# A hand-planned kernel of two attention layers on one core: side products given out by a forecast of their supply

## The chip, the cores and the metric

The kernel runs on one core of a Trainium2 chip. The core has five engines: TensorE (PE, matrix products), VectorE (DVE), ScalarE (ACT), GpSimd (POOL) and SyncE (SP, which here starts DMAs). The metric is the device time of one execution in microseconds (us), and the median of several runs counts.

## What is computed

Four images x of 256 channels and 64 x 64 pixels go through two layers. Each layer first normalizes its input in groups of eight channels and adds its result to that input.

```python
# layer 0: attention of all pixels over a half-sized grid
q = einsum('oc,bchw->bohw', Wq, x)                 # 8 heads of 32
k = conv(x, Wk, strides=(2, 2)); v = conv(x, Wv, strides=(2, 2))
attn = softmax((q.k + q.(rel_h + rel_w)) * scale)  # 4096 queries, 1024 keys
x = x + attn @ v
# layer 1: attention inside each quarter of the image
q, k, v = split(conv1x1(x, w_qkv, b_qkv))
out = softmax(q.k * scale) @ v                     # 1024 queries, 1024 keys, 4 areas
out = out + depthwise_conv7x7(v, w_pe, b_pe)
x = x + conv1x1(out, w_proj, b_proj)
```

(The lines are shortened; q, k and v stand for the normalized input's products.) All numbers are 32-bit floats.

## The kernel before, in words

**Units, steps and phases.** The work is eight blocks: layer 0 of images 0 to 3 ("A"), then layer 1 of images 0 to 3 ("B"). A block has 16 units; a unit is 512 queries of four heads (a head group, `qd` 0 or 1). A unit has 8 steps, one for each 128 of its 1024 keys: 128 units, 1024 steps. The main loop at the end of `direct_path` goes in phases of one and a half steps, 683 in all (`PHASES`). A phase does, in this order for TensorE: the score products `s` of one full step and half of another (L365); the weighted sums `av` of the phase before (L432); and between the two a place for other products. ACT makes the exponentials of the scores (L407 for a full step, two of them, and L418 for a half step), 1024 columns each. DVE adds the exponentials up for the divisors (`acc`, L442).

**PSUM.** It has eight banks. Six hold scores in three pairs (`ps_banks`). One has the tag `av` and holds the running sum of a unit; one has the tag `side` and holds whatever side product is being made (`ps_side`). When a unit's sums are complete, `evict` copies the bank out on ACT (L1055), and only then can the next unit's sums begin in it. In some phases the sums handled belong to two units; `cut` is then not zero, and the order is: sums of the old unit, its eviction, the place for side products, sums of the new unit.

**Side products.** Keys (`make_k`), values (`make_v`, `values`), queries (`make_q`), the output projection (`project`) and the depthwise convolution written as products with band matrices (`convolve`, L979) are generators, cut into parts: two parts for a product of 512 columns or for a convolution of 16 channels, four parts for a key or value product of layer 0. `task` puts one into the list `side`, with its number of parts, a due unit and a test `ready`. `choose` takes the ready task with the earliest due time; a task that has begun is ended before another is taken, since there is one bank. `advance` does one part. `need` forces a task to be done when its result is read.

**How many parts a phase gets.** `pressure` returns how many ready parts wait (`waiting`) and the largest ratio of parts to phases left before they are due (`rate`). If the sums for a unit's divisors are complete, the phase makes the divisors (`den`, L451) and nothing else. Otherwise it gives two parts (four at a rate above 2) when the phase is cut, more than nine parts wait or the rate is above 1; none when at most two wait, nothing has begun and the rate is below 1; and else one, or none, one or two at a unit's edge.

**Divisors.** After `den`, ACT copies it out, and POOL's queue sends it through memory and back twice (rows, few, recs, rb: L469 to L480), with a reciprocal on DVE in between. DVE multiplies the unit's sums by the result two units later (L483). DVE, ACT and each queue work strictly in the order of the program.

**The plan.** `at(g, j, f)` puts a call into step j of unit g. It is used for loads (SP), statistics (`add_stats`, DVE), normalizations (`later`, taken one per phase by `norm_next`, ACT), residual adds, and the calls of `task`. `plan_a` sets the times of layer 0, `plan_b` those of layer 1, `plan_values` those of the values that the convolution reads, and `plan_conv` those of the convolution. What has a negative unit runs before the loop: for image 0 the statistics, all keys and values, and the first queries, and for image 1 the loading for its statistics. There each product takes one of the score pairs, and TensorE runs through them in order. In layer 0 the keys of both head groups become visible together, when the last of the second group's products is in place and the position terms have been added (L548, L549).

**Convolution.** Each `convolve` uses two shares (a band matrix and rows of values for eight channels), loaded by `load_share` through SP's queue into tiles that earlier convolutions free (L960 and L738).

Of the kernel before, what the change touches and what calls it, by code (L numbers as in the profile page):

```python
# [60 lines left out]
def direct_path(  # L61
# [108 lines left out]
    turn = [0]  # L170
# [23 lines left out]

    def task(parts, f, *args, due, ready=None):

        side.append([parts, f(*args), False, ready, due * NKT])

# [40 lines left out]
    def later(token, f, start=0, first=False):  # L239

        if now[0] < 0:
            f()
            norm_done[token] = -1
        else:
            norms_left.insert(0 if first else len(norms_left), (token, f, start))
# [248 lines left out]
    def plan_a(b, u, prep):  # L494
# [3 lines left out]
        early = prep - (5 if b else 0)  # L498
# [13 lines left out]
        def load(a):  # L512
            fetched["a", a] = phase[0]
            areas[a] = [first[2 * a + half] if b == 0 else load_chunk(b, 2 * a + half, "xa") for half in range(2)]
# [58 lines left out]
        plan_norm(key, early + 4 if b != 1 else 0, 3 if b > 1 else 1)  # L573
        for a in range(NAREA):
            g = prep + (2 + 3.4 * a if b else 6 + 2.2 * a)
            at(0, int(NKT * (g - 2.1)), lambda a=a: load(a))
            for n in range(8):
                at(0, int(NKT * (g - 1.6)) + n, lambda a=a, n=n: later(("taps", b, a), lambda: make_taps(a, n), fetched["a", a] + 4))
            for n in range(2):
                at(0, int(NKT * (g + 0.6 * n)), lambda a=a, n=n, g=g: task(4, make_k, a, n, due=min(g + 3.5, u), ready=normed("taps", b, a)))  # L580
                at(0, int(NKT * (g + 0.6 * n + 1.2)), lambda a=a, n=n, g=g: task(4, make_v, a, n, due=min(g + 4, u), ready=normed("taps", b, a)))
# [3 lines left out]
        def fetch(c):  # L585
            fetched["q", c] = phase[0]
            hqs[c] = load_chunk(b, c, "hq")
# [32 lines left out]
        for c in range(NCH):  # L620
# [6 lines left out]
            for qd in range(2):  # L627
                at(g - 2, 4, lambda c=c, qd=qd, g=g: task(2, make_q, c, qd, due=g - 0.5, ready=normed("hq", b, c)))
# [7 lines left out]
                lambda: need(ks, key),  # L636
# [7 lines left out]
    def plan_b(b, u):  # L644
# [66 lines left out]
        for a in range(NAREA):  # L711
# [4 lines left out]
            for n in range(4):  # L716
                at(g - 4, 1 + 4 * n, lambda a=a, n=n, g=g: task(2, make_k, a, n // 2, n % 2, due=g - 1, ready=normed("hs", b, a)))
# [3 lines left out]
        for c in range(NCH):  # L721
            for qd in range(2):
                at(u + 2 * c - 2, 1, lambda c=c, qd=qd: task(2, make_q, c, qd, due=u + 2 * c - 0.5, ready=normed("hs", b, c // 2)))
# [74 lines left out]
        for c in range(NCH):  # L798
# [12 lines left out]
            for to in range(CT):  # L811
                at(g, j + 2, lambda c=c, to=to, g=g: task(2, project, c, to, due=g + 1.6))
# [67 lines left out]
    def plan_values(b, c, start):  # L880
# [50 lines left out]
        for t in range(CT):  # L931
            at(0, when + 7, lambda t=t: task(
                2, values, t, due=start + 2.5, ready=lambda: written[-2] + 4 <= phase[0] and normed("hv", b, c)()
            ))
# [64 lines left out]
    def plan_conv(b, n, start):  # L999
# [4 lines left out]
        def ready():  # L1004
            return all(k in loaded and loaded[k][2] + 4 <= phase[0] for k in ((b, 2 * n), (b, 2 * n + 1)))

        at(0, when, lambda: task(2, convolve, b, n, due=start + 1.5, ready=ready))
# [75 lines left out]

    f = step = 0
    before = []
    while f < PHASES or before or plan or side or quick or norms_left or to_add or to_divide:
# [17 lines left out]
        waiting, rate = pressure()  # L1104
        if due and not begun():
# [23 lines left out]
        norm_next()  # L1129
        if before:  # L1130
# [601 lines left out]
```

## Time and profile before

| | us |
|---|---|
| median of 3 runs | 3141.38 (3141.13 to 3144.78) |
| the profiled execution | 3138.1 |
| its span, first to last instruction | 3136.3 |
| TensorE busy | 3058.4 (98%) |
| VectorE busy | 2517.6 (80%) |
| ScalarE busy | 2456.8 (78%) |
| mean granted TensorE clock | 0.997 |
| the main loop's first score product | 81.6 |
| the main loop's last phase begins | 3104.1 |

The page lists busy time for each engine, groups of instructions by line with a mean duration and the idle time ahead of them, and waits by who released them. Two things are to be kept in mind. Matmuls are pipelined, and a matmul that is held up inside is drawn longer, so a busy TensorE need not be at its peak. And a share of busy time is a mean over stretches with different limits. Times in the timeline count from the span's start.

### The profile page before, as it was taken

How to read it: one execution, taken by the hardware profiler on the slowest of the kernel's cores; microseconds unless marked ns; L12 is line 12 of the kernel's file. 1: busy time of each engine (PE TensorE's matmuls, PEld its weight loads, DVE VectorE, ACT ScalarE, POOL GpSimd, SP SyncE). 2: the span in 40 equal slices, each digit the busy share in tenths (PEclk: the TensorE clock that was granted, in tenths of full speed). 3: DMA queues.
4: the chain of work that ended last, by engine and by line, in shares of the span. 5: the costliest groups of instructions: out<-in, count | busy, mean ns of one | idle time of the engine just before them, and what ended most of it. 6: DMA issues, size and time to landing. Idle time of an engine off the chain costs nothing.

```text
span 3136.3 us, 109812 instructions
## 1 busy us (share of the span) xinstructions
PE 3058.4 (98%) x47138; PEld 1247.9 (40%) x47138; DVE 2517.6 (80%) x2719; ACT 2456.8 (78%) x2988; POOL 486.4 (16%) x923
## 2 busy tenths in 40 slices
PE   7999999999999999999999999999999999999997
PEld 4344433344344444334334444443333444433332
DVE  3788888878787777878778888888887888888888
ACT  2888888888787878878877777788877777778875
POOL 0111111111111111111111111111111111111111
PEclk9999999999999999999999999999999999999999
DMA  5243444556455646566777666665666556633212
GB/s 186 55 96 80 117 97 97 119 109 152 116 155 141 172 133 166 121 158 171 197 187 189 161 173 164 156 178 126 133 130 154 141 156 173 176 103 85 65 44 70
DMA packets 648322, 423.70 MB, mean 135 GB/s; under 512 B 411772, under 2 KB 556636, under 8 KB 647832
## 3 DMA queue, kind: packets, MB, share of 16 engines
q1 hardware_dynamic: 619384, 380.11, 48.0%
q0 software_dynamic: 28448, 36.48, 4.7%
q8 instruction: 378, 6.19, 0.9%
q14 instruction: 112, 0.92, 0.1%
HBM read 318.32 MB, written 98.09 MB: 133 GB/s over the span
## 4 chain that ended last, share of the span: by engine, by line
PE 46%; issue 4%; DMA 2%; DVE 1%; ACT 1%; POOL 1%; SPq 0%; ACTq 0%; POOLq 0%; DVEq 0%
PE s L365 16%; PE av L432 13%; PE q1ps L165 4%; PE ops L165 4%; PE k1ps L165 3%; PE conv_ps L979 2%; PE den L451 2%; PE vals_ps L165 1%; DMA recs<-few 1%; DVE acc L442 1%; ACT p L407 1%; POOL rb L480 0%; SPq L738 0%; DMA xm<-xmid 0%; DMA rb<-recs 0%
## 5 line engine op out<-in xcount | busy, mean ns | idle before, releaser
L442 DVE TENSOR_TENSOR acc<-acc,p 128x1024 f32<-128x1024 f32 x1790 | 2114.1, 1220 | 448.2 <-PE av L432 188.0
L407 ACT ACTIVATE p<-s 128x1024 f32<-128x1024 f32 x1194 | 1160.1, 1025 | 455.6 <-PE s L365 441.3
L418 ACT ACTIVATE p<-s 128x1024 f32<-128x1024 f32 x598 | 620.0, 1037 | 4.0 <-issue 1.8
L365 PE MATMUL s<-q,k_A 32*64 32x256 f32 (+1 forms) x10928 | 557.8, 498 | 11.1 <-ACT p L407 8.1
L365 PE MATMUL s<-q,k_B 32*64 32x512 f32 (+1 forms) x10912 | 548.6, 497 | 2.7 <-ACT p L407 2.1
L432 PE MATMUL av<-p,v_A 128*32 128x256 f32 (+1 forms) x4784 | 455.6, 487 | 0.0
L432 PE MATMUL av<-p,v_B 128*32 128x512 f32 (+1 forms) x4776 | 451.2, 487 | 0.0
L365 PEld LDWEIGHTS s<-q,k_A 32*64 32x64 f32 x10928 | 255.9, 130 | 355.5 <-issue 129.5
L365 PEld LDWEIGHTS s<-q,k_B 32*64 32x64 f32 x10912 | 259.0, 130 | 344.6 <-issue 135.8
L480 POOL DMA_DIRECT2D rb<-recs x508 | 252.0, 502 | 522.4 <-DMA recs<-few 433.2
L478 POOL DMA_DIRECT2D recs<-few x127 | 70.0, 551 | 1394.8 <-DVE sums L477 1225.6
L432 PEld LDWEIGHTS av<-p,v_B 128*32 128x32 f32 x4776 | 148.5, 110 | 262.1 <-issue 236.5
L432 PEld LDWEIGHTS av<-p,v_A 128*32 128x32 f32 x4784 | 149.2, 110 | 241.1 <-issue 202.7
L407 ACT ACTIVATE acc<-s 128x1024 f32<-128x1024 f32 x172 | 166.9, 1023 | 78.0 <-PE s L365 77.8
L451 PE MATMUL den<-acc,ones 128*32 128x512 f32 x1024 | 147.1, 610 | 8.6 <-DVE acc L442 7.6
L470 POOL DMA_DIRECT2D few<-rows x127 | 72.3, 569 | 434.8 <-DMA rows<-den_sb 428.5
L165 PE MATMUL ops<-cv,wp_sb 128*32 128x512 f32 x1024 | 125.4, 604 | 5.2 <-DVE cv L750 4.4
L165 PE MATMUL k0ps<-taps,wkv 128*32 128x256 f32 x2048 | 124.5, 385 | 2.5 <-ACT taps L329 2.5
L165 PE MATMUL q1ps<-h,wqkv_sb 128*32 128x512 f32 x1024 | 123.8, 598 | 1.9 <-ACT q L707 1.9
L165 PE MATMUL vals_ps<-hv,wqkv_sb 128*32 128x512 f32 x1024 | 123.8, 598 | 0.2 <-ACT gmean_A L300 0.2
L165 PE MATMUL k1ps<-h,wqkv_sb 128*32 128x512 f32 x1024 | 123.5, 598 | 0.0
L165 PE MATMUL q0ps<-hq,wq_sb 128*32 128x512 f32 x1024 | 122.8, 597 | 0.0
(99 smaller groups left out, 2128.8 us busy)
## 6 DMA issues: line engine op xcount, KB each, us to landing
rows<-vals SPq DMA_DIRECT2D x384, 195.9 KB
rb<-recs POOLq DMA_DIRECT2D x508, 64.0 KB, 3.0
share<-vals SPq DMA_DIRECT2D x128, 195.9 KB
vala<-vout SPq DMA_DIRECT2D x128, 144.0 KB
vals<-vout SPq DMA_DIRECT2D x128, 144.0 KB
vc<-vala SPq DMA_DIRECT2D x64, 288.0 KB
band<-mats SPq DMA_DIRECT2D x96, 176.0 KB
hq<-in_x SPq DMA_DIRECT2D x32, 512.0 KB
```

The costliest lines, as they stand in the source:

```text
L165: T.matmul(out[cols, :], lhsT=lhsT[:, cols], rhs=rhs, start=start, stop=stop)
L365: T.matmul(out[n : n + WIDE], lhsT=unit[2]()[rows, unit[0], j * P + n : j * P + n + WIDE], rhs=unit[1]()[rows, cols], start=True, stop=True,)
L407: S.activation(p, (a, b)[n], AF.Exp, scale=SCALE)
L418: S.activation(p, c.rearrange("p b (l n) -> p b l n", l=2), AF.Exp, scale=SCALE)
L432: T.matmul(out, lhsT=v[:, j, unit[0] * P + HD * h : unit[0] * P + HD * h + HD], rhs=rhs, start=(j == 0 and not u), stop=(j == NKT - 1), sk ...
L442: V.tensor_add(to, to, p)
L451: T.matmul(dens[g][HD * h : HD * h + HD, :], lhsT=ones, rhs=p(h), start=(n == 0), stop=(n == len(sets) - 1),)
L470: G.dma_start(few[:, 0, :], rows.rearrange("h (q n) -> (h q) n", n=CH // HD))
L478: G.dma_start(recs.rearrange("h (q n) -> (h q) n", n=CH // HD), few[:, 1, :])
L480: G.dma_start(rb[HD * h : HD * h + HD, :], recs[h : h + 1, :].to_broadcast([HD, CH]))
L979: T.matmul(ps[HD * m : HD * m + HD, (2 * k + i) * size : (2 * k + i + 1) * size].rearrange("p (y x) -> p y x", y=NY), lhsT=band[:, half].r ...
```

## The change

It does the following, and leaves every product and its operands as they are.

- **Supply.** `task_at` enters each task, with the phase in which it is expected, into `upcoming`. `supply` adds up the parts that are ready or to come over each horizon of 1 to 24 phases, divides each sum by 13/16 of the phases in it, and takes the least. The loop gives two, one or no part by `credit` plus the larger of supply and rate, each up to 2; what is left over goes into `credit` (between -0.5 and 0.5).
- **Banks.** The tags `av` and `side` become `banks`, two tags; in a cut phase that gives no part and has no task begun, the two change roles.
- **Keys by head group.** The keys of layer 0 become visible for each head group by itself. Three key products of image 0's second group (12 parts) are held back and put into `side` when the loop begins, due at unit 0.6.
- **The plan.** Starting units, due times and lags of loads, statistics, taps, keys, values and convolutions change. In the first 12 phases up to two more normalizations are taken in a phase that gives more than two parts.

```diff
-    turn = [0]
+    turn, banks = [0], ["m0", "m1"]
...
-        return psum.tile([P, CH], FP, tag="side", name=name, bufs=1)
+        return psum.tile([P, CH], FP, tag=banks[1], name=name, bufs=1)
...
+    def task_at(step, parts, f, *args, due, ready=None, lag=1):
+
+        expected = [step * 2 // 3 + 1 + lag, parts]
+        upcoming.append(expected)
+
+        def give():
+            upcoming.remove(expected)
+            task(parts, f, *args, due=due, ready=ready)
+
+        at(0, step, give)
+
+    def supply():
+
+        far = 24
+        comes = [0] * (far + 1)
+        chained = 0
+        for parts, _, started, ready, _ in side:
+            if started or ready is None or ready():
+                comes[0] += parts
+            elif ready.__name__ == "chained":
+                chained += 5
+                comes[min(chained, far)] += parts
+            else:
+                comes[1] += parts
+        for when, parts in upcoming:
+            if when - phase[0] <= far:
+                comes[max(when - phase[0], 1)] += parts
+        total, least = 0, 4.0
+        for h in range(far):
+            total += comes[h]
+            least = min(least, total / max(1, (h + 1) * 13 / 16))
+        return least
...
-        early = prep - (5 if b else 0)
+        early = prep - (5 if b == 1 else 7 if b else 0)
...
-                if qd == 1:
-                    ks[key] = k
+                ks["A", b, qd] = k
...
-        plan_norm(key, early + 4 if b != 1 else 0, 3 if b > 1 else 1)
+        plan_norm(key, early + 4, 3 if b > 1 else 4 if b else 1)
         for a in range(NAREA):
-            g = prep + (2 + 3.4 * a if b else 6 + 2.2 * a)
-            at(0, int(NKT * (g - 2.1)), lambda a=a: load(a))
+            g = prep + (1 + 3.6 * a if b == 1 else 0.05 + 3.7 * a if b else 6 + 2.2 * a)
+            at(0, int(NKT * (g - 2.4)), lambda a=a: load(a))
...
+                if b == 0 and a and n:
+                    held.append((4, make_k, a, n))
+                else:
+                    task_at(int(NKT * (g + 0.6 * n)), 4, make_k, a, n, due=min(g + 3.7, u) if a < 3 or not n else u + 0.3, ready=normed("taps", b, a))
+                task_at(
+                    int(NKT * (g + 0.6 * n + 1.2)), 4, make_v, a, n, due=min(g + 4.2, u - 0.2), ready=normed("taps", b, a)
+                )
...
-                lambda: need(ks, key),
+                lambda n=n: need(ks, ("A", b, n % 2)),
...
-            plan_values(b, c, (18.4, 45.5, 54.5, 84.5)[b] + (1.7, 0.8, 1.3, 1.2)[b] * c)
+            plan_values(b, c, (18.4, 43, 52, 72)[b] + (1.7, 0.9, 1.4, 1.7)[b] * c)
         for n in range(C // 16):
-            plan_conv(b, n, (33, 55.2, 71, 97)[b] + (0.9, 0.95, 0.95, 1.0)[b] * n)
+            plan_conv(b, n, (35, 54.5, 70.5, 89)[b] + (1.2, 0.95, 1.1, 1.5)[b] * n)
...
-            av_of[g] = psum.tile([P, CH], FP, tag="av", name="av", bufs=1)
+            av_of[g] = psum.tile([P, CH], FP, tag=banks[0], name="av", bufs=1)
...
+    for parts, g, *args in held:
+        task(parts, g, *args, due=0.6)
     f = step = 0
-    before = []
+    before, credit = [], 0.0
...
-        waiting, rate = pressure()
+        _, rate = pressure()
+        parts = 0
         if due and not begun():
...
-            waiting = 0
-        elif cut or waiting > 9 or rate > 1 or due or f >= PHASES:
-            side_parts(4 if rate > 2 else 2)
-        elif waiting <= 2 and not begun() and rate < 1:
-            pass
-        elif boundary(mine):
-            side_parts(1 if begun() else 2 if waiting >= 4 else 0)
         else:
-            side_parts(1)
+            wanted = credit + max(min(supply(), 2.0), min(rate, 2.0))
+            if rate > 2:
+                parts = side_parts(4)
+            elif rate > 1.5 or due or f >= PHASES or wanted >= (0.8 if cut else 1.5):
+                parts = side_parts(2)
+            elif wanted >= 0.5 and not cut or begun():
+                parts = side_parts(1)
+            credit = max(-0.5, min(wanted - parts, 0.5))
+            if cut and not parts and not begun():
+                banks.reverse()
...
         norm_next()
+        for _ in range(max(parts, 2) - 2 if f < 12 else 0):
+            norm_next()
```

The rest of the diff turns the other calls of `task` into `task_at`, with due times that are 0.2 to 1.5 units later for most of them (`make_q`, the keys of layer 1, `project`, `values`, `convolve`), and lets what was normalized or loaded before the loop count as ready in the first phase.

More of the change, by code (lines that the diff above doesn't have):

```diff
@@ L193, in direct_path @@
     phase = [0]
+    upcoming, held = [], []
     def task(parts, f, *args, due, ready=None):
         side.append([parts, f(*args), False, ready, due * NKT])
+    def task_at(step, parts, f, *args, due, ready=None, lag=1):
[25 more added lines that the diff above has]
+        return least
     def choose():
@@ L242, in later @@
             f()
-            norm_done[token] = -1
+            norm_done[token] = -2
         else:
@@ L512, in load @@
         def load(a):
-            fetched["a", a] = phase[0]
+            fetched["a", a] = phase[0] if now[0] >= 0 else -4
             areas[a] = [first[2 * a + half] if b == 0 else load_chunk(b, 2 * a + half, "xa") for half in range(2)]
@@ L572, in plan_a @@
             at(early + c // 2, 4 * (c % 2) + (6 if b else 3), lambda c=c: add_stats(c))
-        plan_norm(key, early + 4 if b != 1 else 0, 3 if b > 1 else 1)
+        plan_norm(key, early + 4, 3 if b > 1 else 4 if b else 1)
         for a in range(NAREA):
-            g = prep + (2 + 3.4 * a if b else 6 + 2.2 * a)
-            at(0, int(NKT * (g - 2.1)), lambda a=a: load(a))
+            g = prep + (1 + 3.6 * a if b == 1 else 0.05 + 3.7 * a if b else 6 + 2.2 * a)
+            at(0, int(NKT * (g - 2.4)), lambda a=a: load(a))
             for n in range(8):
-                at(0, int(NKT * (g - 1.6)) + n, lambda a=a, n=n: later(("taps", b, a), lambda: make_taps(a, n), fetched["a", a] + 4))
+                at(0, (max(int(NKT * (g - 1.9)), 3) if b else int(NKT * (g - 1.6))) + n, lambda a=a, n=n: later(("taps", b, a), lambda: make_taps(a, n), fetched["a", a] + 4))
             for n in range(2):
-                at(0, int(NKT * (g + 0.6 * n)), lambda a=a, n=n, g=g: task(4, make_k, a, n, due=min(g + 3.5, u), ready=normed("taps", b, a)))
-                at(0, int(NKT * (g + 0.6 * n + 1.2)), lambda a=a, n=n, g=g: task(4, make_v, a, n, due=min(g + 4, u), ready=normed("taps", b, a)))
+                if b == 0 and a and n:
[5 more added lines that the diff above has]
+                )
         xcs, hqs, made_q = {}, {}, {}
         def fetch(c):
-            fetched["q", c] = phase[0]
+            fetched["q", c] = phase[0] if now[0] >= 0 else -4
             hqs[c] = load_chunk(b, c, "hq")
@@ L627, in plan_a @@
             for qd in range(2):
-                at(g - 2, 4, lambda c=c, qd=qd, g=g: task(2, make_q, c, qd, due=g - 0.5, ready=normed("hq", b, c)))
+                task_at(NKT * (g - 2) + 4, 2, make_q, c, qd, due=g - 0.3, ready=normed("hq", b, c))
             at(g + 3, 0, lambda c=c: load_residual(c))
@@ L716, in plan_b @@
             for n in range(4):
-                at(g - 4, 1 + 4 * n, lambda a=a, n=n, g=g: task(2, make_k, a, n // 2, n % 2, due=g - 1, ready=normed("hs", b, a)))
+                task_at(
+                    NKT * (g - 4) + 1 + 4 * n, 2, make_k, a, n // 2, n % 2, due=g - 0.4, ready=normed("hs", b, a)
+                )
             for n in range(4):
@@ L722, in plan_b @@
             for qd in range(2):
-                at(u + 2 * c - 2, 1, lambda c=c, qd=qd: task(2, make_q, c, qd, due=u + 2 * c - 0.5, ready=normed("hs", b, c // 2)))
+                task_at(
+                    NKT * (u + 2 * c - 2) + 1, 2, make_q, c, qd, due=u + 2 * c - 0.5, ready=normed("hs", b, c // 2)
+                )
         rest, made_x = {}, {}
@@ L811, in plan_b @@
             for to in range(CT):
-                at(g, j + 2, lambda c=c, to=to, g=g: task(2, project, c, to, due=g + 1.6))
+                task_at(NKT * g + j + 2, 2, project, c, to, due=g + (2.2 if b < B - 1 else 3), lag=0)
         return [
@@ L931, in plan_values @@
         for t in range(CT):
-            at(0, when + 7, lambda t=t: task(
-                2, values, t, due=start + 2.5, ready=lambda: written[-2] + 4 <= phase[0] and normed("hv", b, c)()
-            ))
+            task_at(
+                when + 7, 2, values, t, due=start + 4,
+                ready=lambda: written[-2] + 4 <= phase[0] and normed("hv", b, c)(), lag=1 + 4 * t,
+            )
     loaded = {}
@@ L1003, in plan_conv, with chained @@
             at(0, when - 8, lambda: len(loaded) < room and load_share(True))
-        def ready():
+        def chained():
             return all(k in loaded and loaded[k][2] + 4 <= phase[0] for k in ((b, 2 * n), (b, 2 * n + 1)))
-        at(0, when, lambda: task(2, convolve, b, n, due=start + 1.5, ready=ready))
+        task_at(when, 2, convolve, b, n, due=start + 2.5, ready=chained, lag=3)
     units = []
```

## The prediction

> **What bounds the kernel now.** I read the page's busy shares first, then PE's timeline phase by phase (a phase is one turn of the main loop: 1.5 steps of scores, exponentials and weighted sums, and what side products the loop adds), then the waits, then windows for the granted clock.
>
> ```profile
> PE 3058.4 (98%) x47138; PEld 1247.9 (40%) x47138; DVE 2517.6 (80%) x2719; ACT 2456.8 (78%) x2988; POOL 486.4 (16%) x923
> ```
>
> TensorE looks full. Is it full everywhere? PE's timeline over phases that carry two side parts (columns: start, length, engine, line, operation):
>
> ```profile
> 2235.97 1.58 PE L365 MATMUL s<-q,k_B 32*64 32x256 f32 x32
> 2237.48 1.92 PE L165 MATMUL vals_ps<-hv,wqkv_sb 128*32 128x512 f32 x16
> 2239.22 1.47 PE L432 MATMUL av<-p,v_B 128*32 128x512 f32 x16
> 2240.62 1.58 PE L365 MATMUL s<-q,k_B 32*64 32x256 f32 x32
> 2242.13 1.92 PE L165 MATMUL k1ps<-h,wqkv_sb 128*32 128x512 f32 x16
> 2243.87 1.47 PE L432 MATMUL av<-p,v_B 128*32 128x256 f32 x16
> ```
>
> From one first score product to the next: 2240.62 - 2235.97 = 4.65 us, without a gap. Now a stretch in which the loop gave out no side product:
>
> ```profile
> 473.81 2.00 PE L365 MATMUL s<-q,k_A 32*64 32x256 f32 x32 [0.17 <-ACT p L407]
> 475.74 1.50 PE L432 MATMUL av<-p,v_A 128*32 128x256 f32 x16
> 477.17 1.89 PE L365 MATMUL s<-q,k_A 32*64 32x256 f32 x32
> 478.99 1.50 PE L432 MATMUL av<-p,v_A 128*32 128x512 f32 x16
> 480.42 1.93 PE L365 MATMUL s<-q,k_A 32*64 32x256 f32 x32
> 482.27 1.50 PE L432 MATMUL av<-p,v_A 128*32 128x256 f32 x16
> 483.70 1.89 PE L365 MATMUL s<-q,k_A 32*64 32x256 f32 x32
> 486.11 1.76 PE L451 MATMUL den<-acc,ones 128*32 128x512 f32 x5 [0.52 <-DVE acc L442]
> ```
>
> These phases last 3.25 to 3.36 us. PE is drawn as busy, but the same 32 score products take 1.89 to 2.00 us, not 1.58: they are waiting inside. The first window below shows by whom: ACT is busy 13.30 of 13.30 us (and DVE 13.06). So the bound changes with the filling of a phase.
>
> ```profile
> 470.40:483.70 13.30, 13.13 (x196) 4.13 (x192) 13.06 (x13) 13.30 (x18) 2.75 (x6) 1.00 0.34 81
> 853.90:857.10 3.20, 2.04 (x36) 0.54 (x32) 3.10 (x3) 3.20 (x6) 0.00 (x0) 1.00 0.88 273
> 857.10:863.70 6.60, 4.98 (x24) 1.12 (x24) 3.13 (x6) 3.03 (x5) 1.92 (x4) 0.74 0.23 85
> ```
>
> (Columns: window, its length, busy time of PE, weight loads, DVE, ACT, POOL; granted clock, DMA share, GB/s.)
>
> I cut the whole trace into its 683 phases at the first score product. Medians: two parts 4653 ns (413 phases), one part 3799 (61), divisors and no part 3794 (127). So a part costs PE 854 ns, divisors 849, and the rest of a phase 3799 - 854 = 2945. The 66 phases with nothing should take 2945; outside the start they take 3.2 to 3.4, or 4.2 to 4.6 where one unit's sums end inside the phase ("cut"):
>
> ```profile
> 1893.02 1.58 PE L365 MATMUL s<-q,k_B 32*64 32x256 f32 x32
> 1894.53 0.64 PE L432 MATMUL av<-p,v_B 128*32 128x256 f32 x8
> 1896.67 1.07 PE L432 MATMUL av<-acc,v_B 128*32 128x512 f32 x8 [1.50 <-ACT av_sb L1055]
> 1897.66 1.58 PE L365 MATMUL s<-q,k_B 32*64 32x256 f32 x32
> ```
>
> The new unit's sums go to the bank that ACT still has to empty, and no side product lies between.
>
> I charge each phase with what it lasts above 2945 + 854 per part + 849 for divisors. That excess is 96 us of the 3136.3 us span; it is all that a better distribution could win:
> - 38.0 us in the phases without a part: 19.8 in 54 plain ones (5 at the start), 18.2 in 12 cut ones.
> - 27.2 us in phases at most three behind such a phase. Four short phases leave DVE no room (its accumulating adds take 2114 / 683 = 3.1 us a phase), so the next divisors wait for it; ACT pays its debt as 0.42 us in the next full phase.
> - 31.0 us with no empty phase near: DVE or DMA late at 1545 to 1580 us (about 8), at 405 to 430 and 498 to 510 us, ACT's eviction in one-part cuts.
>
> The dearest single wait:
>
> ```profile
> 858.70 2.10 PE L451 MATMUL den<-acc,ones 128*32 128x512 f32 x5 [2.76 <-DVE acc L442]
> ```
>
> **A rule that speaks against the change.** The Trainium skill (Perfetto Trace Analysis, "Identifying the Most-Contended Engine") says matmul occupancy is a bad measure of PE's load and that the share of weight loads should be read instead. By it PE stands at 40%, DVE at 80% is the bound, and giving out PE's work more evenly is worth about 0. The rows decide otherwise: 854 ns more for each part, in 413 phases alike, is an engine without slack. Only the empty phases obey ACT and DVE.
>
> **The change, part by part.**
>
> *Even giving out (supply, credit, expected tasks).* Parts in the loop: 948 in this trace, 12 more after the change, and the phases not used by divisors are 683 - 127 = 556: 960 / 556 = 1.73 parts each. Per 16 units (about 69 such phases), from the diff's start units, tasks that become available: 108, 128, 138, 114, 138, 132, 118, 84, so 1.2 to 2.0 a phase; no stretch is below one. A phase with one part already costs exactly PE's time (median excess 0), so "0 2 0 2" made into "1 1 1 1" gains the whole excess of the zeros. Readiness is bunched, so I leave about 12 empty phases at 0.3 to 0.4: 5 us remain of 38.0. **Gain 33.**
>
> *The debts behind empty phases*, 27.2 us. The wait at 858.70 belongs here: empty and full phases in turn up to it, then 2.76 us of waiting, and then the matmuls run at half pace (granted clock 0.74 in the window above), 6.05 us of excess in all. The skill (TensorE: Matmul & The Clock Gate, Part 1) puts the fall to half clock behind an idle window of about 3.4 us. By that rule this wait costs 2.8 us; by the row 6.0. I take the row. The pair at 1386 to 1396 us (3.2 + 1.4) I leave standing: ACT waits 4.4 us there for the load of hv, a DMA matter, and then the clock falls too. With 1.6 of others, 6 us remain. **Gain 21.**
>
> *The others*, 31.0 us. What hangs on one-part cuts, on group statistics asked for too late (phases 99 to 101 and 169, 4.8 us) and on layer 0's late four-part products (405 to 430 us, 2.9) is moved by the earlier statistics and later due times. What hangs on transposes, position adds and DMA stays. **Gain 9.**
>
> *Banks change roles* in a cut phase without a part: the 1.50 us wait falls to ACT's pace (0.36). It overlaps the 18.2 above, and is not counted twice.
>
> *A new cost.* The loop now gives out single parts more often, and a part begun must be ended before another task: some cut phases get one part, which covers the eviction badly. Two such cuts stand in the trace, excess 0.42 and 0.85. There are about 85 cuts; an eighth at 0.63: **7 us lost** (0 if none falls so, 25 if 40 do).
>
> *Keys by head group; three key products held.* Before the loop PE runs without a gap from 20.6 to 80.9 us, 3.45 us for each key or value product, so 3 x 3.45 = 10.4 us leave it; the loop gets 12 x 0.854 = 10.2. Net nothing but the filled phases 0 to 5 (3.9 us, in the 33). The second group is first read in phase 5; rate is above 2, so four parts go into each of phases 0, 1, 2. Its two position adds (1.22 each) come beside DVE's adds in phases of 6.4 us: hidden, 2.4 us if not.
>
> *Moved steps.* For images 2 and 3 eight loads of xs and sixteen statistics (0.68 each, 10.9 us of DVE) come two units earlier; the first image's convolution two units later and slower (1.2 units apart, was 0.9), so it now runs into the values of images 1 and 2; the values of images 1 and 2 come 2.5 units earlier, the last image's values 12.5 and its convolution 8. Layer 0's taps, keys and values of images 1 to 3 come one or two units earlier, so they are no longer late before their first use. Bytes stay. All go through SP's one queue, where share loads wait for their convolution (433.7 us on conv_ps L979), so whatever stands behind waits too; the POOL chain for divisors shares the DMA engines. Between 43 and 53 units the DMA share was 0.62 and will rise; at 60 to 64 it hardly changes. I take 0 net; bounds -8 (waits at 1545 to 1580 us ease) and +15 (three more waits like that of 858.70).
>
> *Extra normalizations in phases 0 to 11:* 0.6 us of ACT each in phases of over 4.6 us: nothing.
>
> Sum: 33 + 21 + 9 - 7 = **56 us**. The profiled execution took 3138.1 us (span 3136.3): 3082. The median of the runs, 3141.4, is 3.3 above it: **3085 us**.
>
> **Rivals.**
> - *DVE and DMA keep their waits (24%).* Only the empty phases go, the debts reappear where ACT, DVE or DMA are late anyway: 33 from the first, 7 from the second, -7: 3108. For it: DVE at 80% overall, 0.86 DMA share at 1540 to 1580 us. Against it: the debts sit behind empty phases.
> - *The moved plan clears the other waits too (13%).* Remaining excess about 17: 3062.
> - *Supply dries up (5%).* Tasks are listed but not ready, the rate rule saves too much or phases stay empty; only the changed banks gain 12 x 1.2: 3127.
> - *Slower (6%).* The first image's convolution, now beside values from 43 to 53 units, makes divisor chains, hv loads and shares late, and each such wait, as that of 858.70, costs 6 by the half clock. It decides from ten of them, 10 x 6 = 60 against 56 gained; with 15, one in 1.7 units, 3141 - 56 + 90 = 3175.
>
> **How the numbers follow.** Even filling 52% at 3085, own range 3070 to 3098. The 80% range takes in most of the two neighbours, 3058 to 3114; outside it are dried-up supply, slower, and tails. A measurement here tells 0.2% (6 us) from no change: faster 0.93, same 0.02, slower 0.05.
>
> **What would show it.** In the trace after: under 15 phases without a part; two-part phases still 4653 ns and one-part 3799; PE waits for av_sb under 5 us (16.5 now); the loop's first scores at 71 us, not 81.6; granted clock 1.00 around 860 us. Wrong: many phases still empty; new waits of PE on DVE acc or of ACT on hv between 43 and 69 units; one-part cuts with 0.4 to 0.85 us each in large number.

## The result, and the profile after

| | before | after |
|---|---|---|
| median on the same chip, us | 3141.38 (7 runs, 3137.8 to 3146.5) | 3124.0 (7 runs, 3120.7 to 3131.7) |
| the profiled execution | 3138.1 | 3122.4 |
| its span | 3136.3 | 3120.7 |
| the loop's first score product | 81.6 | 71.4 |
| the loop's last phase begins | 3104.1 | 3089.9 |

The ratio is 0.9949 (95% interval 0.9934 to 0.9964): faster by half a per cent, 16 us. The forecast was 3085, and its range ended at 3114: the sign was right, the size was not. The page's busy shares, which answer to the first line of the prediction, hardly show it:

```profile
PE 3046.9 (98%) x47138; PEld 1258.4 (40%) x47138; DVE 2517.8 (81%) x2719; ACT 2455.8 (79%) x2988; POOL 484.1 (16%) x923
```

PE is at 98% before and after, with the same number of instructions. The timeline has to say what became of the empty phases. This is PE's timeline of the kernel after, at the place where before gave out nothing (columns as in the prediction):

```profile
465.32 1.58 PE L400 MATMUL s<-q,k_A 32*64 32x256 f32 x32
466.82 1.92 PE L165 MATMUL q0ps<-hq,wq_sb 128*32 128x512 f32 x16
468.57 1.47 PE L467 MATMUL av<-p,v_A 128*32 128x512 f32 x16
469.97 1.58 PE L400 MATMUL s<-q,k_A 32*64 32x256 f32 x32
```

469.97 - 465.32 = 4.65 us, scores at 1.58 us: a full phase at PE's own pace. The stretch that ran at ACT's pace is gone.

I counted the excess over 2945 + 854 per part + 849 for divisors in the same way for both traces (a slightly refined count gives 98.0 us for before, where the prediction had 96):

| excess, us | before | after | forecast |
|---|---|---|---|
| phases without a part | 37.8 (65 of them) | 4.1 (17) | 5 (12) |
| at most three phases behind one | 26.8 | 11.8 | 6 |
| no empty phase near | 33.4 | 69.5 | 22, and 7 for one-part cuts |
| sum | 98.0 | 85.4 | 40 |

The first row did what was forecast, 33.7 us. The third more than doubled. Of its 69.5 us, about 11 are one-part cuts (16 of them, median 0.85), and some 37 are nine phases: at 698 (5.8), 1246 (1.6), 1348 (6.9), 1475 (1.1), 1513 (5.5), 2122 to 2145 (5.1, 3.9, 5.2) and 2173 us (2.7). In eight of them PE stands still, for 0.7 to 4.6 us; the ninth, at 2132 us, runs at half clock behind the wait ahead of it.

The granted clock in the trace is 0.50 for 3.4 us from 702.9, for 6.8 us each from 1354.9, 1518.7 and 2133.1, and for 3.4 us from 2150.2: 27.3 us in the main loop, where before has 10.2 (3.4 each from 859.8, 1392.3 and 1580.0). At half speed up to 13.7 us are lost there, against 5.1. At 1246, 1475 and 2173 us the clock stays at 1.00; the last of these phases gives out eight parts at once and waits twice 0.81 us for ACT's copies of keys, not for a load.

One of the nine, in PE's timeline after (brackets: idle time before, and who ended it):

```profile
1349.63 0.46 PE L1023 MATMUL conv_ps<-rows,band 88*32 88x128 f32 x8
1350.39 0.89 PE L1023 MATMUL conv_ps<-rows,band 88*32 88x128 f32 x24 [0.30 <-DMA rows<-vals]
1353.14 0.46 PE L1023 MATMUL conv_ps<-rows,band 88*32 88x128 f32 x8 [1.86 <-DMA rows<-vals]
1355.69 1.52 PE L1023 MATMUL conv_ps<-rows,band 88*32 88x128 f32 x24 [2.09 <-DMA rows<-vals]
1356.95 2.81 PE L467 MATMUL av<-p,v_A 128*32 128x256 f32 x16
```

The convolution has begun before its rows are there: three waits for rows, of 0.30, 1.86 and 2.09 us, and then, at half clock, sums that take 2.81 us instead of 1.47. SP's timeline shows the loads (columns: start, length of the issuing, queue, line, operation, number):

```profile
1337.57 3.17 SPq L1007 DMA_DIRECT2D rows<-vals  x4
1342.68 4.68 SPq L1007 DMA_DIRECT2D rows<-vals  x4
```

The second group of four (the convolution's second share) is issued from 1342.68 to 1347.36; the convolution begins at 1349.63, 2.3 us later, and its last wait ends at 1355.69, 8.3 us after the last of these loads was issued. The program counts a share as ready four phases after the call that loads it; SP's queue does not know of phases.

The stretch at 2122 us, PE's timeline after and the windows for its clock (columns of the windows as in the prediction):

```profile
2127.19 1.02 PE L1023 MATMUL conv_ps<-share 88*32 88x128 f32 x25 [2.01 <-issue]
2132.12 3.19 PE L400 MATMUL s<-q,k_B 32*64 32x256 f32 x32 [2.62 <-ACT p L442]
2135.24 3.64 PE L165 MATMUL ops<-cv,wp_sb 128*32 128x512 f32 x16
```

```profile
2122.30:2132.10 9.80, 5.19 (x116) 3.13 (x112) 5.42 (x8) 2.82 (x4) 0.55 (x1) 1.00 0.70 177
2132.10:2140.70 8.60, 8.51 (x67) 2.07 (x68) 8.46 (x9) 4.53 (x5) 2.56 (x5) 0.60 0.75 146
```

Two waits of 2.01 and 2.62 us, then a granted clock of 0.60, with scores of 3.19 us where 1.58 is usual and a projection of 3.64 where 1.92 is. The waits make the phase at 2122 us 5.1 us too long, the clock the one at 2132 us 3.9: the second price is nearly as high as the first. DVE's and ACT's timelines tell what was waited for at that time:

```profile
2125.56 0.71 DVE L726 STREAM_TRANSPOSE v_B<-vc 128x512 f32<-128x512 f32 x1 [10.89 <-DMA vc<-vala]
2131.04 1.02 ACT L442 ACTIVATE p<-s 128x1024 f32<-128x1024 f32 x1 [6.49 <-DVE acc L477]
```

DVE works in the program's order, so while the transpose waits for vc, its adds for the divisors stand for 10.89 us and longer; ACT then waits 6.49 us for an add, and PE 2.62 us for ACT. SP issued those two vc loads at 2117.50. The wait at 2145 us (3.66 us) is for DVE's `xm`, the residual add.

Three lines of the waits after (engine and line, waited for: total, times, longest, in us):

```profile
PE av L467 <- ACT av_sb L1099: 9.2, 18, 1.3
...
PE conv_ps L1023 <- DMA rows<-vals: 7.7, 5, 2.4
...
PE den L486 <- DVE acc L477: 2.8, 1, 2.8
```

and the same three of before:

```profile
PE av L432 <- ACT av_sb L1055: 16.5, 15, 1.8
...
PE den L451 <- DVE acc L442: 7.6, 6, 2.8
...
PE conv_ps L979 <- DMA rows<-vals: 1.1, 1, 1.1
```

What the change went for fell (7.6 to 2.8, 16.5 to 9.2), and a wait for transfers rose from 1.1 to 7.7 us. The DMA share rose where the forecast said so, and beyond it: in units 52 to 56 from 0.64 to 0.77, in 76 to 80 from 0.63 to 0.77, in 88 to 92 from 0.55 to 0.63.

### The profile page after: what moved, and what is told of

Its sections match the earlier page's. It is cut to its first block, busy times and chain, and to the rows that moved or that the text cites. A ratio compares the mean times of both kernels' runs of the same rounds, so it can differ in the third digit from the quotient of the medians.

```text
span 3120.7 us, 109786 instructions
## 1 busy us (share of the span) xinstructions
PE 3046.9 (98%) x47138; PEld 1258.4 (40%) x47138; DVE 2517.8 (81%) x2719; ACT 2455.8 (79%) x2988; POOL 484.1 (16%) x923
## 5 line engine op out<-in xcount | busy, mean ns | idle before, releaser
L400 PE MATMUL s<-q,k_A 32*64 32x256 f32 (+1 forms) x10928 | 548.0, 498 | 4.4 <-ACT p L442 2.1
L486 PE MATMUL den<-acc,ones 128*32 128x512 f32 x1024 | 140.3, 608 | 2.8 <-DVE acc L477 2.8
```

The lines of the kernel that those rows point to most:

```text
L400: T.matmul(out[n : n + WIDE], lhsT=unit[2]()[rows, unit[0], j * P + n : j * P + n + WIDE], rhs=unit[1]()[rows, cols], start=True, stop=True,)
L486: T.matmul(dens[g][HD * h : HD * h + HD, :], lhsT=ones, rhs=p(h), start=(n == 0), stop=(n == len(sets) - 1),)
```

## The experiments

Three theories stood at the start. **The starts:** the new starting units of values and convolutions put transfers on top of one another. **The waits re-form:** whatever is given out more evenly, PE reaches a late transfer sooner, and the sum of waits comes back somewhere else. **The margin:** a share counts as ready after a number of phases, while SP's in-order queue runs behind; the new rule takes a task as soon as it counts as ready, so a margin that was slack before is now used up.

All ratios below are to the kernel before, on the same chip, with a 95% interval. "Excess" is counted as in the table above.

### One part of the change undone

**Starts of before in the kernel after:**

```diff
-            plan_values(b, c, (18.4, 43, 52, 72)[b] + (1.7, 0.9, 1.4, 1.7)[b] * c)
+            plan_values(b, c, (18.4, 45.5, 54.5, 84.5)[b] + (1.7, 0.8, 1.3, 1.2)[b] * c)
...
-            plan_conv(b, n, (35, 54.5, 70.5, 89)[b] + (1.2, 0.95, 1.1, 1.5)[b] * n)
+            plan_conv(b, n, (33, 55.2, 71, 97)[b] + (0.9, 0.95, 0.95, 1.0)[b] * n)
```

> The changed kernel with the starting units of values and convolutions as before the change; giving out by supply, bank roles, held keys and all else as changed. Theory 1 (the new starts make transfers collide: DMA share rose from 0.56 to 0.67 at units 44-48, 0.63 to 0.77 at 52-56, 0.62 to 0.76 at 76-80, and the new waits of 37 us stand there): the waits at 1348, 1513 and 2122-2145 us go, about 3095 to 3105 us. Theory 2 (the even giving out itself leaves transfers and DVE too little room, wherever the tasks start): waits of the same sum stand elsewhere, about 3120 to 3130 us.

Measured: 3131.2 us, 0.9992 (0.9983 to 1.0000). Excess 85.5 us, as much as after, in a profiled execution that was the fastest of 13 and 6.0 us below their median; the waits stand elsewhere, at 813, 1344 to 1382, 1529 and 2359 us. The even giving out, with the rest of the plan but without the new starts, gains next to nothing, so the starts are not what spoils it. The first theory falls as the main cause.

**The old rule for the number of parts in the kernel after** (no supply, no credit, no change of banks; starts, held keys and due times stay new):

```diff
-            wanted = credit + max(min(supply(), 2.0), min(rate, 2.0))
-            if rate > 2:
...
+            if cut or waiting > 9 or rate > 1 or due or f >= PHASES:
+                parts = side_parts(4 if rate > 2 else 2)
+            elif waiting <= 2 and not begun() and rate < 1:
+                pass
...
```

> The changed kernel with the rule of before for the number of parts (ready parts and rate; no supply, no credit, no change of bank roles); starts, held keys and due times as changed. Theory 1: the new starts alone cost, so slower than the kernel before or equal: 3140 to 3165 us, with waits of convolutions for rows. Theory 2: without the even giving out there are no new waits, 3125 to 3140 us.

Measured: 3124.5 us, 0.9966 (0.9954 to 0.9978). Excess 85.8, of it 15.8 in empty phases. The new plan alone gives two thirds of what the whole change gives. With the transfers as they are, the rule that clears 11.7 us more of empty phases (15.8 to 4.1) adds 0.0017, and the intervals overlap. The stretch at 2121 to 2142 us stands in this kernel too: that one does come with the new starts (with the starts of before it is absent).

### The waits one by one

**The loads of xs for images 2 and 3 half a unit sooner:**

```diff
-            at(early + c // 2, 4 * (c % 2), lambda c=c: look(c))
+            at(early + c // 2, 4 * (c % 2) - (4 if b > 1 else 0), lambda c=c: look(c))
```

> The changed kernel with the loads of xs for images 2 and 3 issued four steps earlier, statistics where they were. If DVE's in-order wait for xs (3.9 us) makes the wait of the divisors at 698 us and the half clock behind it (5.8 us of excess), that goes: about 3118 us. If the transfers of that stretch are late whatever is issued when, no change: 3124.

Measured: 3120.4 us, 0.9958 (0.9945 to 0.9972), the same as after; excess 91.1. In the queue's own waits between 650 and 712 us, this kernel has

```profile
SPq L108 <- DVE st_A L543: 23.2, 2, 14.1
```

where the kernel after has

```profile
SPq L108 <- DVE st_A L543: 8.3, 2, 6.0
```

The load can't go sooner: its tile, one of six, is freed by DVE's statistics. SP stands at it for 14.1 us instead of 6.0, and what is queued behind it stands too. An earlier start in the program only lengthened a wait. (A seventh tile wasn't tried.)

**A share counts as ready six phases after its load, not four:**

```diff
-            return all(k in loaded and loaded[k][2] + 4 <= phase[0] for k in ((b, 2 * n), (b, 2 * n + 1)))
+            return all(k in loaded and loaded[k][2] + 6 <= phase[0] for k in ((b, 2 * n), (b, 2 * n + 1)))
```

> The changed kernel, but a convolution counts as ready six phases after its shares are issued, not four. Theory 1: PE no longer waits inside a convolution for rows (7.7 us, with the half clock behind it 15 us at 1246, 1348, 1475, 1513 us): about 3109 us. Against it: the next shares are issued only by a convolution, so the chain of shares gets longer, convolutions come late and the wait moves to where they are read: 3120 to 3135 us.

Measured: 3106.2 us, 0.9911 (0.9897 to 0.9924), apart from the interval of after and the best version with all its work. Excess 66.3. The convolution that waited three times, in this kernel's PE timeline:

```profile
1343.87 1.99 PE L1023 MATMUL conv_ps<-rows,band 88*32 88x128 f32 x64
```

All 64 products in one run. From the end of the issue of a share's last rows to their first use, waits included, the least time is 11.2 us, where after has 4.9 (before 6.5). The margin theory gains 0.38%.

**The vc loads through ACT's queue instead of SP's:**

```diff
-            nc.sync.dma_start(vcs[a, n], vala[b][a][...])
+            S.dma_start(vcs[a, n], vala[b][a][...])
```

> The changed kernel with the loads of vc (values of layer 1 for the transposes) started by ACT's queue, not SP's. Theory 3 (a step of the plan counts phases of the program, but SP's queue in order runs behind it: vc was issued at 2117.5 us, some 16 us late, and DVE waited 10.9 us for it): DVE's wait for vc goes, and with it the waits of 5.1, 3.9 and 5.2 us at 2122 to 2145 us, about 3110 us. Rival (the 16 DMA engines are full there, whoever issues): vc lands no earlier, 3120 to 3126 us.

Measured: 3153.2 us, 1.0059 (1.0046 to 1.0073), slower than before. DVE's wait for vc went, but the stretch behind it stays (11.9 us of excess from 2122 to 2147), and ACT, in whose queue the loads now are, shows new waits; the longest:

```profile
ACT hv L364 <- DMA cv<-conv: 11.7, 1, 11.7
```

This is ACT's timeline there, and SP's:

```profile
2019.75 0.33 ACTq L719 DMA_DIRECT2D vc<-vala  x1
2020.12 0.81 ACT L364 ACTIVATE hv<-hv,norm_B 128x512 f32<-128x512 f32 x1 [11.73 <-DMA cv<-conv]
```

```profile
2011.19 11.81 SPq L781 DMA_DIRECT2D cv<-conv  x16
```

The normalization of hv doesn't read cv. ACT stands ahead of the vc load, from 2008.39 on; the load's issue then takes 0.33 us. In the trace this load waits for semaphore 102, the one that it raises itself when it lands, and that semaphore was raised last by a cv load which SP issued only at 2016.86 and which landed at 2019.73. The program's transfers from SP and ACT take turns on eight semaphores, and 1563 of 2132 wait for the earlier transfer on their own. So the vc loads left SP's queue but not its order, and the wait for that order now stands on the exponentials' engine. What a load free of SP's order would gain was not tried. The DMA share in those 12 us was 0.60.

### What the parts are worth once the convolutions don't wait

Three kernels on top of the margin of six. **Single parts only where they don't leave a product half done at a unit's edge:**

```diff
-                parts = side_parts(1)
+                even = not begun() or side[0][0] % 2 == 0
+                parts = side_parts(2 if boundary(mine) and even else 1)
```

> The kernel with readiness after six phases (e4_ready6), and a single part in the phase ahead of a cut only when it ends a task that has begun or leaves an even rest. Prices the new cost of the forecast: 15 cut phases with one part cost 10.7 us in e4_ready6; if that is their price, 3098 us. If ACT's copy of the finished sums is waited for in a cut phase with two parts or none as well, no change: 3106.

Measured: 3112.1 us, 0.9921 (0.9907 to 0.9935). The one-part cuts, 10.7 us of excess, are gone, and 15 empty cuts take 5.4; three phases at 699, 1901 and 2123 us carry 3.3 to 5.1 us. No gain: the empty phases in all rise from 5.7 to 10.5 us, and what stands behind them from 16.2 to 23.3.

**The banks keep their roles:**

```diff
-                banks.reverse()
+                pass
```

> e4_ready6 without the change of bank roles. Six cut phases without a part would wait 1.3 to 1.7 us again for ACT's copy, not 0.23: about 7 us slower, 3113 us. If few such phases are left, since giving out fills them, no change.

Measured: 3110.3 us, 0.9924 (0.9911 to 0.9938). Six empty cuts now cost 8.8 us (median 1.41 each) instead of 1.6: the roles are worth 7.2 us by the profile and 4.1 by the ratios. The intervals overlap.

**The three key products before the loop again:**

```diff
-                if b == 0 and a and n:
+                if False and b == 0 and a and n:
```

> e4_ready6 with the three key products before the loop, as before the change. The loop starts 10.4 us later and has 12 parts (10.2 us) less; only the empty phases at the start come back, 2 to 4 us: 3108 to 3110 us. If the held products themselves made the first phases wait for DVE or ACT, faster: 3103.

Measured: 3113.5 us, 0.9937 (0.9924 to 0.9951). The first score product is at 83.0 us again, and the empty phases take 10.1 instead of 5.7. The held keys are worth 8 us by the ratios, whose intervals touch, 4.4 of it in filled phases; the forecast had 3.9.

### The margin everywhere

If the margin is the cause, all the tests that count phases should gain by six instead of four (taps, queries, hv, values, shares). One edit, in four kernels:

```diff
-                    ("hq", b, c), lambda: norm_chunk(c, t), fetched["q", c] + 4, True
+                    ("hq", b, c), lambda: norm_chunk(c, t), fetched["q", c] + 6, True
...
-                ready=lambda: written[-2] + 4 <= phase[0] and normed("hv", b, c)(), lag=1 + 4 * t,
+                ready=lambda: written[-2] + 6 <= phase[0] and normed("hv", b, c)(), lag=1 + 4 * t,
...
```

In the kernel after:

> The changed kernel with every margin that is counted in phases at six, not four: shares to convolution (as in e4_ready6), the store of vout to the next values, and the loads of hv, hq and xa to their normalizations. Theory 3 (a margin of four phases of program order is shorter than SP's queue and the transfers take; the new rule uses a task at once when it is called ready): all of it matters, 3095 to 3103 us. Rival: the convolutions' margin was all, 3104 to 3110; longer margins delay tasks and bring empty phases back, over 3110.

In the kernel after with the starts of before:

> e1_old_starts (new giving out, old starting units of values and convolutions, 3131 us) with every margin at six phases. Theory 3: its waits were late transfers too, so 3100 to 3112 us. Theory 1 (it is where the transfers are put that makes them late): the waits stay, 3122 to 3132.

In the kernel before:

> The kernel before with every margin at six phases and nothing else. Theory 3: the old rule left ready tasks lying (1.1 us of waiting for rows in all), so longer margins give it little: 3125 to 3136 us. Rival: the margin is the whole gain and even giving out is worth nothing: about 3108.

In the kernel after with the old giving out:

> p1_old_giving (old rule for parts, new starting units, 3125 us) with every margin at six phases. Theory 3: some of the waits at 709 and 2121 to 2142 us go, but the empty phases (15.8 us) and what hangs on them stay: 3112 to 3122 us. Rival (even giving out is worth nothing): as m6_after, within 3.

| | margins of four | of six | excess with six |
|---|---|---|---|
| after | 0.9949 (0.9934 to 0.9964) | 3115.4 us, 0.9942 (0.9928 to 0.9955) | 76.8 |
| starts of before | 0.9992 (0.9983 to 1.0000) | 3190.6 us, 1.0180 (1.0167 to 1.0194) | 156.9 |
| before | 1 | 3171.3 us, 1.0120 (1.0104 to 1.0135) | 126.6 |
| old giving out | 0.9966 (0.9954 to 0.9978) | 3131.7 us, 0.9992 (0.9985 to 0.9999) | 89.5 |

"Margins are too short everywhere" falls: in the kernel after it gives nothing, in the others it costs. In the one with the starts of before the waits for transfers move to where the values are written, as its waits show:

```profile
DVE vout L938 <- DMA vals<-vout: 36.4, 7, 5.6
```

A reason that fits, argued and not tested by itself: the old plan puts convolutions 0.9 to 1.0 unit apart, some 5 phases, less than a margin of six. In the kernel before they ran 22.7 to 24.4 us apart, with the longer margins 27.2 to 29.3, so they fall behind their plan. The new starts of two images, 1.2 and 1.5 units apart, leave room for it. With margins of six, giving out evenly costs 19 us on the starts of before (with the rest of the plan) and gains 16 on the new ones: there one lets the other work. With margins of four no such thing can be told: the two by themselves give 3 and 11 us, together 16.

### The loads of shares left out

To see how much of the missing gain hangs on these transfers, four kernels load only the first two shares and use them for every convolution. Their convolution's result is therefore not the reference's; products, order and all other transfers stay.

```diff
-    loaded = {}
+    loaded, stock = {}, []
...
+        if len(stock) == 2:
+            loaded[b, k] = *stock[k % 2], phase[0]
+            return
...
+        stock.append((band, xs))
```

In before, after, after with the starts of before, and after with the old giving out:

> The kernel before without the convolutions' loads of shares, all but the first two; these two are used again, so the convolution's result is not the reference's. All products, exponentials and additions stay. Excess of the empty phases stays (38), what hangs on transfers goes (about 12 of 96): 3120 to 3128 us by either theory.

> The changed kernel without the convolutions' loads of shares, all but the first two (the convolution's result is not the reference's). If late transfers ate the gain: the waits at 1246, 1348, 1475, 1513 and 2122 to 2145 us go, 3075 to 3088 us, the forecast's number. If the loss is in the giving out itself: above 3105.

> New giving out with the old starting units of values and convolutions (e1_old_starts), without the loads of shares as in n_after (convolution not the reference's). If transfers alone made it as slow as the kernel before: 3078 to 3095 us. If the old starting units bunch the tasks so that supply dries up: over 3105.

> Old rule for parts with the new starting units (p1_old_giving), without the loads of shares as in n_after (convolution not the reference's). If even giving out is worth 35 to 50 us where no transfer is late: 3112 to 3125 us, near n_before. If the starting units are the gain: near n_after.

| | with the loads | without | excess without |
|---|---|---|---|
| before | 1 | 3125.5 us, 0.9958 (0.9941 to 0.9975) | 84.1 |
| after | 0.9949 (0.9934 to 0.9964) | 3090.9 us, 0.9850 (0.9834 to 0.9867) | 53.3 |
| starts of before | 0.9992 (0.9983 to 1.0000) | 3112.6 us, 0.9920 (0.9903 to 0.9936) | 74.4 |
| old giving out | 0.9966 (0.9954 to 0.9978) | 3108.8 us, 0.9907 (0.9891 to 0.9924) | 63.6 |

Without these loads the change gains 3125.5 - 3090.9 = 34.6 us, with them 16. Giving out evenly gains 12.9 us on the starts of before (3125.5 to 3112.6, with the rest of the plan) and 17.9 on the new ones (3108.8 to 3090.9). The loads cost the kernel before 0.42%, 13 us, and the kernel after (0.9949 - 0.9850) x 3138 = 31 us: **18 us of the gain are lost there**, give or take 9 by the three intervals. That is the largest single piece of the 39 us that are missing, and it is shown, not argued.

The phases say the same. The third row of the excess falls from 69.5 to 37.3 us in the kernel after, and only from 33.4 to 22.1 in the one before. Of the nine phases seven are gone, 29.3 us, those that waited for vc and `xm` among them; the one at 698 us, behind late xs, keeps 4.4 of 5.8 us, and the one with eight parts its 2.7. The half clock in the loop falls from 27.3 to 6.8 us.

What these runs don't separate: with the loads, their bytes go, and so does the time that SP's queue stands until a convolution frees a share's tile (in the kernel after 333.3 us on conv_ps at L1004, behind which all later loads stand too).

Of the four expectations, that for before holds, and the kernel after lies 3 us above its first branch, with the waits gone as expected. With the starts of before, 3112.6 us is in the branch "over 3105", but not for want of supply: the empty phases take only 7.6 us there. Products come in bunches: phases that give out six to ten parts at once (at 815, 1347 and 2348 us), with the one at 1358 us, carry 16.6 us. The old giving out, 3108.8, lies between its two branches: both pieces gain.

**Even parts again, with the loads left out too** (the two edits above together, in the kernel after):

> n_after (no loads of shares but the first two; the convolution's result is not the reference's), and a single part in the phase ahead of a cut only when it ends a task or leaves an even rest, as in e6_ready6_even. If one-part cuts cost what they show (11.1 us, and 3 to 4 come back in cuts without a part at 0.23 each): 3081 to 3084 us on the chip where n_after had 3090.9, a ratio of about 0.982 to before. If the wait only moves: 0.985.

Measured: 3089.2 us, 0.9855 (0.9840 to 0.9871), against 0.9850 without the edit. One-part cuts (11.1 us of excess) gone, empty cuts with 5.0 us come; with these, the empty phases rise from 4.1 to 8.6 us and what stands behind them from 11.9 to 16.3. The price of a one-part cut stands in the profile, but most of it moved, and no gain in time was to be had. A one-part cut, in PE's timeline after:

```profile
3013.39 0.64 PE L467 MATMUL av<-p,v_B 128*32 128x256 f32 x8
3013.84 1.04 PE L165 MATMUL ops<-cv,wp_sb 128*32 128x512 f32 x8
3015.53 1.06 PE L467 MATMUL av<-acc,v_B 128*32 128x512 f32 x8 [0.64 <-ACT av_sb L1099]
```

The one part takes 1.04 us, and ACT's eviction ends 0.64 later.

**A margin of five for the shares** (as the edit of six, with `+ 5`):

> The changed kernel with a convolution ready five phases after its shares are issued (four as changed: ratio 0.9949; six: 0.9911). If the length of the margin acts: about 0.993, 3112 us. If six helped by shifting the convolutions' transfers against other loads: near 0.995 or any other value outside that.

Measured: 3121.7 us (3109.6 to 3127.8), 0.9947 (0.9928 to 0.9966): nothing gained on four. The waits at the convolutions are gone (the least time from issue to use is 9.5 us), but the stretches at 1479 (5.1), 1936 (9.2) and 2124 to 2147 us (15.3 together) stand. So six phases don't win by clearing the convolutions alone; they also shift all later loads, and happen to part those that met. With seven no run was made.

## Why the prediction was wrong, point by point

- **What bounds the kernel: right.** A second part costs 854 ns in before and 857 in after (medians 4653 and 3796), at PEld 40% and DVE 81%. By the share of weight loads (the Trainium skill, Perfetto Trace Analysis, "Identifying the Most-Contended Engine"; the page names the share of peak arithmetic beside it, which the prediction leaves out) the change would have been worth nothing; without the shares' loads it is worth 34.6 us.
- **Empty phases, 33: right.** 37.8 to 4.1 us, 17 phases left where 12 were forecast.
- **Debts, 21: too high.** 26.8 to 11.8, so 15. The wait of 858.70 us itself went, but the like of it, DVE's acc late by 2.76 us, stands at 703.53, behind statistics whose xs are late; there it isn't made by empty phases.
- **Banks: right in kind.** An empty cut costs 0.23 us each in after (forecast 0.36); without the roles 1.41.
- **One-part cuts, 7: too low.** 16 cuts, median 0.85, 11.1 us; forecast 11 at 0.63. They cost something, but taking them away gains no time (0.9855 against 0.9850).
- **Held keys: right.** The loop begins at 71.4 us; the filled phases gain 4.4 (3.9 forecast).
- **The others from 31 to 22, and "I take 0 net" for the moved steps, "bounds -8 and +15": this step failed.** The row rose from 33.4 to 69.5 us, at most 11 of it one-part cuts. Set against 22, that is about 36 us too many, of a total of 45 (85.4 against 40); the debts have 6 and the cuts 4. With +36 us it lies far outside the bounds. In its place the runs without the loads of shares show what the moved and denser steps cost: 18 us of time, and by phases 32 of the row's 69.5 us in after against 11 of 33.4 in before, hang on these loads. The rest isn't assigned, save 4.4 us behind late xs and 2.7 in the phase with eight parts.
- **Why it failed.** The forecast asked what the moved steps cost by themselves, and took the margins of the program as given. The margins are counted in phases. A loop that takes a task as soon as it counts as ready leaves less time between issue and use (least 6.5 us before, 4.9 after), and the starts that were moved raise the DMA share there. That the loads of shares are late is shown; that the margin's length is the reason is not, since with five phases the waits at the convolutions go and the time stays. A long wait costs twice, by itself and by the clock: half clock takes up to 13.7 us in after's loop, 5.1 in before's.
- **The rival "Slower" had the mechanism.** Late shares and loads at some 6 us each, ten of them to lose all. By its own price, 3085 + 6 x 6 = 3121, if the nine phases with their 37 us count as six such waits; that this lands so near 3124 is in part luck, since debts and cuts missed by another 10. It was given 6% as an outcome of many such waits, and none as a term of the sum. The place was right for 1246 us (unit 50), nearly for 1348 (unit 54), and not for 698, 1513 and 2122. "DVE and DMA keep their waits", 3108, had the right direction, and too little.
- **The signs named beforehand.** One- and two-part phases (3796 and 4653 ns), the loop's start and the clock at 860 us came as said. The empty phases are 17, not under 15, and PE's waits for av_sb 9.2 us, not under 5: most of them stand in one-part cuts.

What stays open: which transfers have to be kept apart. Four and five phases give 0.9949 and 0.9947, six 0.9911, six everywhere 0.9942; each shifts the whole order of loads, and no run here tells the placement from the length, nor the bytes of the loads from the standing of SP's queue. Nor was the wait for xs taken away.

## What to carry to other kernels

When a schedule is made denser, every margin that counts steps of the program in place of time is a suspect: list, from the trace of before, the time from the end of a load's issue to its first use, and put a price on each that is near the time to land (in the case shown here rows were waited for until 8.3 us after their issue). Work out a rival's mechanism as a term of the sum too: "how many of these, if not ten?" And to learn what a class of transfers costs, run the kernel without them, before and after: the difference of the two differences is what the change loses there, with the noise of all three ratios in it.

## What had not been expected of the hardware

- The granted clock fell after waits shorter than thought. The Trainium skill (TensorE: Matmul & The Clock Gate, Part 1) speaks of an idle window of about 3.4 us; here two waits of 2.01 and 2.62 us with 2.3 us of products between, or 1.86 and 2.09 with 0.46 between, were enough for 0.60 and 0.62 in the next 8 us. A single wait of 2.76 us did it as well (0.74 in the prediction's window), and in the kernel after without the loads of shares one of 2.04 us ahead of 703.83 (0.50 from 704.1 to 707.5). The length alone doesn't decide: in the kernel before with margins of six a wait of 2.91 us ahead of 784.45 was followed by no fall. In all traces of this case every one of the 30 waits of PE in the loop over 3.0 us was, and the falls last 3.41 us or a multiple of it.
- A load can hold the engine that starts it, though its issue is short: ACT stood 11.7 us ahead of a vc load whose issue took 0.33 us, because that load waited for a semaphore that a load in SP's queue had yet to raise. Moving loads to another queue moved the wait onto the exponentials.
- The granted clock differs from run to run of one kernel, and the time with it: the seven runs of the kernel after go from 3120.7 us at a mean granted clock of 0.996 to 3131.7 at 0.992, those with a margin of five from 3109.6 at 0.997 to 3127.8 at 0.993.
